# Layers 2 and 3 of a four-layer graph kernel: TensorE bound to the text's order, with timed chains of small steps between the main products

## The chip, the cores and the metric

The kernel runs on one core of a Trainium2 chip. Its time is the device time of one execution in microseconds (us). The kernel before took 2191.8 us in the median of four runs (2189.2 to 2206.82).

## The reference

Four graph layers follow each other on `x` of shape (8, 2048, 64) with one dense 0/1 matrix `adj` of 2048 x 2048. Each layer normalizes its input, applies relu, and adds its result to the input. The change touches layers 2 and 3:

```python
def _L2_gnn_ref(causal_vars, adj_matrix, intervention_value, W1, b1, W2, b2, idx):
    v = causal_vars.at[:, idx].set(intervention_value)
    for _ in range(3):
        effects = jnp.einsum('nm,bmd->bnd', adj_matrix, v)
        h = jnp.concatenate([v, effects], axis=-1)
        h = jax.nn.relu(jnp.einsum('bnk,dk->bnd', h, W1) + b1)
        v = jnp.einsum('bnk,dk->bnd', h, W2) + b2
    return v

def _L3_gnn_ref(x, A, embedding, weight, bias):   # K = 3
    w = jnp.einsum('nd,dkio->nkio', embedding, weight)
    b = jnp.einsum('nd,do->no', embedding, bias)
    As = [eye, A, 2.0 * (A @ A) - eye]
    x_g = jnp.einsum('knm,bmc->bnkc', jnp.stack(As), x)
    return jnp.einsum('bnki,nkio->bno', x_g, w) + b

# layers 2 and 3
h = jnp.maximum(_layernorm(x, axis=-1), 0.0)
x = x + layer(h, adj, ...)
```

## The kernel before

The eight batches are worked in four passes `p` (NP = 4) of two batches, whose 64 features each fill the 128 partitions. The 2048 nodes are the free dimension, cut into four chunks `c` of 512 (`NCW`, `cols(c)`) or sixteen tiles of 128 (NT). The transposed adjacency matrix stays in SBUF as sixteen tiles `aT[m]`.

Everything here happens in `layers23`, from line 1410. A product with the matrix is `spread` (L1482): for one chunk, sixteen tiles times two parts, since the left operand is split into a rounded part `hi` and the rest `lo`, both in a one-pass float type. So one chunk of a product is 32 matmuls of 128x512 into one PSUM tile `acc`.

A pass has three stages.

- Layer 2, three steps over four chunks. A chunk begins with `acc = W1v` (or `Wvc`) times `v` (L1515), then `spread`, then a relu on ScalarE (ACT) that writes the chunk of `v` in place (L1517). In steps 0 and 1 `moved` (L1454) makes the next left operand: four small matmuls into `py` (L1459), a bias on VectorE (DVE, `yb`, L1466), `hi` on ACT (L1467) and `lo` on GpSimd (POOL, L1468). In step 2 the chunk is finished instead: a product with W2 into `pv`, the sum with x, the store of x3 with the bias of layer 3, the normalization (`norm`), and a transpose (`turned`, L1471).
- The first product of layer 3, into `y1`, with a transpose of each chunk.
- The second product of layer 3 into `y2`. After each chunk, its four tiles go through the `u` stage: a transpose `px` of x (L1555), then two groups `w` of six matmuls of 64 rows (L1564). The two batches' matmuls of a pair use different halves of the rows of TensorE. DVE multiplies by the embedding (L1572) and adds (L1576, L1582), POOL folds (L1583 to L1585), SP stores.

Within that last stage `enter` (L1491) begins the next pass for a chunk: load x, mean (L719), subtract, square, variance (L724), logarithm, exponential, multiply, and `moved` with W1e. Chunk c - 1 enters while chunk c is in its `u` stage. Chunk 3 enters after the last `u`. The first pass enters all four chunks before its first step in the text.

`check` (L1433) also tests the matrix: it loads a 128x512 piece `raw` (256 KB) and lets DVE see whether it holds anything but 0 and 1. Two pieces stand at the start of each chunk of layer 2 until all 64 are done.

The text doesn't set the order in which the engines work. A planner puts each engine's instructions in an order by its own estimates of time, and takes later work when earlier work isn't ready by these estimates. Within an engine the order then is fixed, and every engine works its list in turn. `tc.keep_in_program_order` binds an instruction to the place it has in the text; before the change that is done in the `u` stage only, for five of the six matmuls of each group. Buffers rotate within a tag: `x`, `ca` and `fold` have two, `pr` three, `hi` and `lo` six each. A tile that needs a buffer waits until the tile before it in that buffer has been read. DMAs of this part are issued by SP, in order.

Of the kernel before, what the change touches and what calls it, by code (L numbers as in the profile page):

```python
# [16 lines left out]
P = 128  # L17
# [14 lines left out]
def cols(c, w=CW):  # L32
    return slice(c * w, (c + 1) * w)
# [588 lines left out]
class Kit:  # L622


    def __init__(self, tc, t, pool):
        nc = self.nc = tc.nc
        self.tc, self.t = tc, t
        self.ident = pool.tile([P, P], FP, name="ident_f")
# [57 lines left out]
    def layer2_weights(self, pool, ps):  # L686
# [22 lines left out]
        nc.vector.tensor_copy(self.cb, pw)  # L709

    def use_ln_exp(self):
        self.tc.keep_in_program_order(self.nc.scalar.preload_act_table_set(LN_EXP))

    def norm_steps(self, dst, src, mean, var, xc, q):

        nc, mm = self.nc, self.nc.tensor.matmul
        n = dst.shape[-1] // CW
        for c in range(n):
            mm(mean[:, cols(c)], self.avg, src[:, cols(c)], start=True, stop=True)  # L719
        nc.vector.tensor_sub(xc, src, mean)  # L720
        nc.scalar.activation(q, xc, AF.Square)  # L721
        yield
        for c in range(n):
            mm(var[:, cols(c)], self.avg, q[:, cols(c)], start=True, stop=True)  # L724
        nc.scalar.activation(q, var, AF.Ln, bias=self.eps)
        nc.scalar.activation(q, q, AF.Exp, scale=-0.5)
        nc.vector.scalar_tensor_tensor(dst, xc, 0.0, q, op0=OP.max, op1=OP.mult)
        yield
# [679 lines left out]


def layers23(kit, aT, x2_dram, x3_dram, out):  # L1410

    tc, nc, t = kit.tc, kit.nc, kit.t
    mm = nc.tensor.matmul
    ident, ones = kit.ident, kit.ones
    ctx = ExitStack()
    W1v, W1e, W2, Wvc, Wec, cb = kit.W1v, kit.W1e, kit.W2, kit.Wvc, kit.Wec, kit.cb
    b1, b2c, ivc, b1c = kit.b1, kit.b2c, kit.ivc, kit.b1c
    K3, D3 = 3, 16

    fin = ctx.enter_context(tc.tile_pool(name="f_in", bufs=2, reuse_waits="tile"))  # L1420
    w2 = ctx.enter_context(tc.tile_pool(name="w2f", bufs=1, reuse_waits="tile"))
    sb = ctx.enter_context(tc.tile_pool(name="f_sb", bufs=2, reuse_waits="tile"))
    ps = ctx.enter_context(tc.tile_pool(name="f_ps", bufs=2, space=PSUM, reuse_waits="tile"))

    def norm(dst, src):

        mean = ps.tile([P, CW], FP, tag="tp", name="mean")
        var = ps.tile([P, CW], FP, tag="tp", name="var")
        xc = fin.tile([P, CW], FP, tag="ca", name="xc")
        q = fin.tile([P, CW], FP, tag="q", name="q", bufs=1)  # L1430
        kit.norm(dst, src, mean, var, xc, q)

    def check(n):  # L1433

        for _ in range(n):
            if not todo:
                return
            m, h = todo.pop(0)
            a = sb.tile([P, CW], FP, tag="fold", name="raw")
            nc.sync.dma_start(out=a, in_=t["adjT"][m * P : (m + 1) * P, cols(h)])  # L1440
            k = 7 + NCW * m + h
            nc.vector.scalar_tensor_tensor(  # L1442
                a, a, 0.5, a, op0=OP.is_gt, op1=OP.not_equal, accum_out=kit.bad[:, k : k + 1]
            )

    todo = [(m, h) for m in range(NT) for h in range(NCW)]

    def parts():
        return (
            sb.tile([P, 4, P], FR, tag="hi", name="hi", bufs=6),  # L1450
            sb.tile([P, 4, P], FR, tag="lo", name="lo", bufs=6),
        )

    def moved(v, c, W, bias):  # L1454

        py = ps.tile([P, 4, P], FP, tag="tp", name="py")
        for k in range(4):
            m = 4 * c + k
            mm(py[:, k, :], v[:, m * P : (m + 1) * P], W, start=True, stop=True)  # L1459
        hi, lo = parts()  # L1460
        if bias is None:
            nc.scalar.copy(hi, py)
            nc.vector.tensor_tensor(lo, py, hi.bitcast(FP), op=OP.subtract)  # L1463
        else:
            yb = fin.tile([P, 4, P], FP, tag="ca", name="yb")
            nc.vector.tensor_tensor(yb, py, bias[:, None, :].to_broadcast([P, 4, P]), op=OP.add)  # L1466
            nc.scalar.copy(hi, yb)  # L1467
            nc.gpsimd.tensor_tensor(lo, yb, hi.bitcast(FP), op=OP.subtract)  # L1468
        return hi, lo

    def turned(v, c):  # L1471

        tp = ps.tile([P, 4, P], FP, tag="tp", name="tp")
        for k in range(4):
            m = 4 * c + k
            nc.tensor.transpose(tp[:, k, :], v[:, m * P : (m + 1) * P], ident)
        hi, lo = parts()
        nc.scalar.copy(hi, tp)  # L1478
        nc.vector.tensor_tensor(lo, tp, hi.bitcast(FP), op=OP.subtract)  # L1479
        return hi, lo  # L1480

    def spread(acc, y, c, start):  # L1482

        for m in range(NT):
            for part in y[m // 4]:
                mm(acc, part[:, m % 4, :], aT[m][:, cols(c)], start=start, stop=m == NT - 1 and part is y[m // 4][1])  # L1486
                start = False

    v = fin.tile([P, N], FP, name="v", bufs=1)

    def enter(p, c):  # L1491

        xp = fin.tile([P, CW], FP, tag="x", name="xp")
        nc.sync.dma_start(out=xp, in_=x2_dram[p, :, cols(c)])
        norm(v[:, cols(c)], xp)
        if c == 0:
            nc.vector.tensor_copy(v[:, 0:1], ivc)
        return moved(v, c, W1e, None)

    y = [enter(0, c) for c in range(NCW)]  # L1500
    W3 = w2.tile([P, K3, D3 * F], FP, name="W3f")
# [5 lines left out]
    nc.vector.tensor_sub(W3[:, 0, :], W3[:, 0, :], W3[:, 2, :])  # L1507
    nc.vector.tensor_scalar(W3[:, 2, :], W3[:, 2, :], 2.0, None, op0=OP.mult)
    for p in range(NP):
        for step in range(3):  # L1510
            yn = []
            for c in range(NCW):
                acc = ps.tile([P, CW], FP, tag="acc", name="acc")
                check(2)
                mm(acc, Wvc if step else W1v, v[:, cols(c)], start=True, stop=False)  # L1515
                spread(acc, y, c, False)
                nc.scalar.activation(v[:, cols(c)], acc, AF.Relu, bias=b1c if step else b1)  # L1517
                if step < 2:
                    yn.append(moved(v, c, Wec, cb))
                    continue  # L1520
                pv = ps.tile([P, CW], FP, tag="tp", name="pv")
                mm(pv, W2, v[:, cols(c)], start=True, stop=True)
                xp = fin.tile([P, CW], FP, tag="x", name="xq")
                nc.sync.dma_start(out=xp, in_=x2_dram[p, :, cols(c)])
                nc.vector.scalar_tensor_tensor(xp, pv, b2c, xp, op0=OP.add, op1=OP.add)
                bq = sb.tile([P, CW], FP, tag="pr", name="bq", bufs=3)
                nc.sync.dma_start(out=bq, in_=kit.bias_dram[:, cols(c)])
                nc.gpsimd.tensor_add(bq, bq, xp)
                nc.sync.dma_start(out=x3_dram[p, :, cols(c)], in_=bq)
                norm(v[:, cols(c)], xp)  # L1530
                yn.append(turned(v, c))
            y = yn


        y1 = sb.tile([P, N], FP, tag="y1", name="y1", bufs=1)
        yn, after = [], []
        for c in range(NCW):
            acc = ps.tile([P, CW], FP, tag="acc", name="acc")
            spread(acc, y, c, True)
            nc.scalar.copy(y1[:, cols(c)], acc)  # L1540
            yn.append(turned(y1, c))
        for c in range(NCW):
            acc = ps.tile([P, CW], FP, tag="acc", name="acc")
            spread(acc, yn, c, True)
            y2 = fin.tile([P, CW], FP, tag="ca", name="y2")
            nc.scalar.copy(y2, acc)
            xp = fin.tile([P, CW], FP, tag="x", name="xr")
            nc.sync.dma_start(out=xp, in_=x3_dram[p, :, cols(c)])
            if c > 0 and p + 1 < NP:
                after.append(enter(p + 1, c - 1))  # L1550
            for k in range(4):
                i = 4 * c + k
                ns, ks = slice(i * P, (i + 1) * P), slice(k * P, (k + 1) * P)
                px = ps.tile([P, P], FP, tag="tp", name="px")
                nc.tensor.transpose(px, xp[:, ks], ident)  # L1555
                xs = sb.tile([P, 2, F], FP, tag="xs", name="xs", bufs=1)
                nc.scalar.copy(xs.rearrange("p h f -> p (h f)"), px)
                pr = []
                for w in range(2):
                    u = [ps.tile([P, 8, F], FP, tag=f"u{h}", name=f"u{h}") for h in range(2)]  # L1560
                    for kk, src in enumerate((v[:, ns], y1[:, ns], y2[:, ks])):
                        for h in range(2):

                            one = mm(  # L1564
                                u[h].rearrange("p d o -> p (d o)"), src[half(h), :], W3[half(h), kk, cols(w)],
                                start=kk == 0, stop=kk == 2,
                            )
                            if kk or h:
                                tc.keep_in_program_order(one)
                    for h in range(2):  # L1570
# [6 lines left out]
                        else:  # L1577
                            pr.append(a)
                fold = sb.tile([P, 2, 4, F], FP, tag="fold", name="fold")
                ot = sb.tile([P, 2, F], FP, tag="ot", name="ot", bufs=1)  # L1580
# [7 lines left out]
                )  # L1588
        y = after + [enter(p + 1, NCW - 1)] if p + 1 < NP else None
    ctx.close()  # L1590
# [101 lines left out]
```

## Time and profile before

| | |
|---|---|
| median of four runs | 2191.8 us |
| the profiled execution | 2197.11 us, span 2195.3 us |
| mean granted TensorE clock | 0.981 |
| layers 2 and 3 | from about 993 us to the end |
| last `u` stage's end | about 2184 us |
| raw checks (DVE) | 24 in pass 0, 24 in pass 1, 16 in pass 2, none in pass 3 |

The starts of the first W1v product of the four passes are at 1006.5, 1312.4, 1610.8 and 1907.5 us.

How to read the lines that follow: a row of a group of instructions gives line, engine, operation, output and inputs, shapes and count, then busy time and mean ns of one, then the idle time before. A row of waits gives the waiting instruction, the one it waited for, the total in us, the number of times, and the longest. A row of a stretch gives its borders, its length, the busy time and number of instructions of TensorE (PE), its weight load, DVE, ACT and POOL, then the granted clock, the share of the DMA engines and GB/s. A row of the timeline gives start, length, engine, line, operation, names and shapes, and in brackets the idle time before with what ended it.

### The profile page before, as it was taken

The page shows a single profiled execution, that of the slowest core. Times are in us where ns is not written, and L with a number is a line of the kernel's source. Part 1 is how long each engine was busy: PE and PEld are TensorE (multiplying, and loading weights), DVE is VectorE, ACT ScalarE, POOL GpSimd, SP SyncE. Part 2 cuts the span into 40 slices and gives each one's busy share as a digit, 9 for nine tenths or more (in the row PEclk, how much of TensorE's full clock was granted, in tenths as well). Part 3 has the DMA queues.
Part 4 walks back from the last instruction along what each step waited for, and adds up shares of the span by engine and source line. Part 5 has one row for each costly group of instructions (what it writes and reads, how often), then busy time and mean ns, then how long its engine had stood idle before and what let it go on. Part 6 is the DMA issues. An engine that isn't in the chain of part 4 may idle for free.

```text
span 2195.3 us, 23784 instructions
## 1 busy us (share of the span) xinstructions
PE 2097.5 (96%) x9164; PEld 1158.3 (53%) x9164; DVE 1219.5 (56%) x1890; ACT 451.7 (21%) x852; POOL 297.5 (14%) x416
## 2 busy tenths in 40 slices
PE   7999898888999999998999999999999999999997
PEld 4777655423222222225766547774557664576653
DVE  6675588868888887874223564116551235501265
ACT  4322244464111111002121111120111201112100
POOL 0211154301000000000110121101111011111022
PEclk9999899989999999999999999999999999999999
DMA  4665361154111111104210014000030100101000
GB/s 122 195 202 154 118 212 45 52 164 154 44 34 39 58 34 39 49 20 135 65 43 8 22 37 122 24 20 21 24 100 6 44 10 21 42 1 34 11 19 12
DMA packets 86154, 140.26 MB, mean 64 GB/s; under 512 B 33040, under 2 KB 33296, under 8 KB 83792
## 3 DMA queue, kind: packets, MB, share of 16 engines
q1 hardware_dynamic: 67984, 88.05, 13.5%
q0 software_dynamic: 18048, 50.60, 7.6%
q8 instruction: 74, 1.21, 0.2%
q14 instruction: 48, 0.39, 0.1%
HBM read 107.89 MB, written 30.74 MB: 63 GB/s over the span
## 4 chain that ended last, share of the span: by engine, by line
PE 63%; issue 16%; DVE 6%; DMA 6%; POOL 4%; ACT 2%; POOLq 0%; DVEq 0%; SPq 0%; ACTq 0%
PE acc L1486 19%; PE o L1355 11%; PE u L1564 7%; PE dn L1361 6%; DMA raw<-in_adjT 3%; PE acc L913 2%; PE var L724 2%; PE pgs L1141 2%; PE py L1459 2%; PE mean L719 2%; PE acc L1515 1%; POOL fold L1583 1%; DVE ex L1139 1%; POOL mix L1140 1%; PE ph L1302 1%
## 5 line engine op out<-in xcount | busy, mean ns | idle before, releaser
L1486 PE MATMUL acc<-aT,hi 128*128 128x512 f32 x960 | 402.1, 419 | 0.0
L1486 PE MATMUL acc<-aT,lo 128*128 128x512 f32 x960 | 388.7, 405 | 0.0
L1355 PE MATMUL o<-pt,hS 128*64 128x512 f32 x1024 | 269.9, 608 | 5.8 <-DVE pt L1370 5.8
L1370 DVE SCALAR_TENSOR_TENSOR pt<-R,wd,aT 128x1024 f32<-128x1024 f32 x192 | 239.1, 1280 | 41.4 <-PE dn L1361 22.9
L1564 PE MATMUL u<-W3f,y 64*128 64x512 f32 x1024 | 258.3, 592 | 0.0
L1572 DVE TENSOR_TENSOR pr<-u,embf 128x512 f32<-128x512 f32 x256 | 171.5, 688 | 123.0 <-PE u L1564 110.9
L1486 PEld LDWEIGHTS acc<-aT,hi 128*128 128x128 f32 x960 | 181.0, 189 | 62.1 <-issue 23.5
L1486 PEld LDWEIGHTS acc<-aT,lo 128*128 128x128 f32 x960 | 180.9, 188 | 51.2 <-issue 13.6
L1355 PEld LDWEIGHTS o<-pt,hS 128*64 128x64 f32 x1024 | 70.8, 137 | 188.5 <-issue 174.8
L1564 PEld LDWEIGHTS u<-W3f,y 64*128 64x128 f32 x1024 | 104.4, 187 | 124.6 <-issue 124.6
L1564 PE MATMUL u<-W3f,v 64*128 64x512 f32 x512 | 146.5, 617 | 0.0
L1361 PE MATMUL dn<-pt,vd 128*32 128x512 f32 x1024 | 142.4, 599 | 0.0
L913 PE MATMUL acc<-at,Y 128*128 128x512 f32 x512 | 134.9, 408 | 2.3 <-DVE ev L922 2.3
L1486 PE MATMUL acc<-aTl,lo 128*128 128x512 f32 x320 | 129.7, 406 | 6.2 <-DVE lo L1463 4.5
L1486 PE MATMUL acc<-aTl,hi 128*128 128x512 f32 x320 | 128.4, 402 | 3.4 <-ACT hi L1467 3.4
L1583 POOL TENSOR_TENSOR fold<-fold 128x256 f32<-128x256 f32 x64 | 47.3, 739 | 556.2 <-DVE fold L1582 556.2
L1466 DVE TENSOR_TENSOR yb<-py,cb_f 128x512 f32<-128x512 f32 x32 | 22.1, 690 | 160.7 <-PE py L1459 160.6
L913 PEld LDWEIGHTS acc<-at,Y 128*128 128x128 f32 x512 | 94.0, 192 | 25.1 <-issue 4.2
L721 ACT ACTIVATE q<-xc 128x512 f32<-128x512 f32 (+1 forms) x56 | 38.7, 691 | 266.7 <-DVE xc L720 253.9
L1576 DVE TENSOR_TENSOR pr<-pr 128x512 f32<-128x512 f32 x128 | 88.1, 689 | 2.2
L1479 DVE TENSOR_TENSOR lo<-tp,hi 128x512 fp32r<-128x512 f32 x32 | 22.1, 692 | 117.5 <-ACT hi L1478 117.5
L1442 DVE SCALAR_TENSOR_TENSOR raw<-raw 128x512 f32<-128x512 f32 x64 | 49.1, 772 | 68.9 <-DMA raw<-in_adjT 68.6
(278 smaller groups left out, 2718.7 us busy)
## 6 DMA issues: line engine op xcount, KB each, us to landing
at<-in_adjT POOLq DMA_DIRECT2D x32, 512.0 KB, 4.6
raw<-in_adjT SPq DMA_DIRECT2D x64, 256.0 KB, 3.2
aT<-in_adjT POOLq DMA_DIRECT2D x12, 1024.0 KB, 7.1
R<-r_dram SPq DMA_DIRECT2D x14, 512.0 KB, 3.6
hi_dram<-hi SPq DMA_DIRECT2D x16, 264.0 KB, 2.7
lo_dram<-lo SPq DMA_DIRECT2D x16, 264.0 KB, 3.5
hhi<-hi_dram POOLq DMA_DIRECT2D x16, 264.0 KB, 3.0
hlo<-lo_dram POOLq DMA_DIRECT2D x16, 264.0 KB, 3.1
```

What stands on the lines that cost most here:

```text
L719: mm(mean[:, cols(c)], self.avg, src[:, cols(c)], start=True, stop=True)
L724: mm(var[:, cols(c)], self.avg, q[:, cols(c)], start=True, stop=True)
L913: mm(acc[p], Y[h][:, m, p, :], at[:, k, :], start=m + h == 0, stop=m == NT - 1 and h == 1)
L1355: mm(o[half(b2), cols(k)], hS[:, m, half(b2)], pts[b2][:, cols(k)], start=m == 0, stop=m == NT - 1)
L1361: mm(dn[q : q + 32, :], vd[:, m, b2 : b2 + 1].to_broadcast([P, 32]), pts[b2][:, cols(k)], start=m == 0, stop=m == NT - 1, tile_position=(0 ...
L1370: nc.vector.scalar_tensor_tensor(pt, R[b2], wd[:, m, b2 : b2 + 1], aT[m][:, s].bitcast(FP), op0=OP.max, op1=OP.mult)
L1442: nc.vector.scalar_tensor_tensor(a, a, 0.5, a, op0=OP.is_gt, op1=OP.not_equal, accum_out=kit.bad[:, k : k + 1])
L1486: mm(acc, part[:, m % 4, :], aT[m][:, cols(c)], start=start, stop=m == NT - 1 and part is y[m // 4][1])
L1564: one = mm(u[h].rearrange("p d o -> p (d o)"), src[half(h), :], W3[half(h), kk, cols(w)], start=kk == 0, stop=kk == 2,)
L1572: nc.vector.tensor_tensor(a, u[h], emb[:, i, 8 * w : 8 * w + 8, None].to_broadcast([P, 8, F]), op=OP.mult)
L1576: nc.vector.tensor_add(pr[h], pr[h], a)
L1583: nc.gpsimd.tensor_add(fold[:, :, 0:2, :], fold[:, :, 0:2, :], fold[:, :, 2:4, :])
```

## The change

Every matmul and transpose of layers 2 and 3 goes through `kit.mm` or `kit.turn`, which bind it to the text's order. To make that order, the text is now written by a small clock, `Weave`: the work between main products (entering, carrying, leaving, turning) is written as generators, `chains`, that yield the time after which their next step may stand. `spread` and the `u` stage tell the clock how long they take (0.47 us for two matmuls, 0.93 for the W product, 0.27 and 2.8 in the `u` stage), and steps that are due are put into the text there. `until` puts steps in at once until an operand exists.

Besides this:

- `moved` makes `lo` on DVE in all cases, no longer on POOL where there is a bias.
- `hi` and `lo` of chunks 2 and 3 take buffers of `fold` and `pr` (`LENT`) for the operands made in step 0 and step 2.
- The raw pieces use the two buffers of `x` instead of `fold`, and stand in steps 0 and 1 alone, so 16 in each pass.
- Mean and variance use PSUM of `u0`, `u1` (at the start and in step 2) or of `acc` (in the `u` stage). The tile `q` is gone; the normalization writes into its own output.
- The first pass enters all four chunks before the first product; chunks 2 and 3 are loaded into y1's space.
- In the last chunk's `u` stage the next pass's chunk 3 enters too, in parts of `y1` that are no longer read; after the stage ACT copies it into `v`.
- The first product of layer 3 takes its first two chunks together, tiles 0 to 7, 8 to 11, 12 to 15 of each in turn.
- x for `leave` and for the `u` stage is loaded ahead of the chunk's product.

```diff
+    def mm(self, *args, **kw):
+        one = self.nc.tensor.matmul(*args, **kw)
+        if self.strict:
+            self.tc.keep_in_program_order(one)
...
+class Weave:
+    def __init__(self):
+        self.now, self.chains = 0.0, []
+    def start(self, chain):
+        self.chains.append([self.now + next(chain), chain])
+    def step(self, c):
+        d = next(c[1], None)
+        if d is None:
+            self.chains.remove(c)
+        else:
+            c[0] = self.now + d
+    def passed(self, us):
+        self.now += us
+        for c in list(self.chains):
+            if c[0] <= self.now:
+                self.step(c)
+    def until(self, there):
+        while not there():
+            c = min(self.chains, key=lambda c: c[0])
+            self.now = max(self.now, c[0])
+            self.step(c)
...
-            a = sb.tile([P, CW], FP, tag="fold", name="raw")
+            a = fin.tile([P, CW], FP, tag="x", name="raw")
...
+    LENT = (None, None, ("fold", 2), ("pr", 3))
...
-            nc.gpsimd.tensor_tensor(lo, yb, hi.bitcast(FP), op=OP.subtract)
...
+        nc.scalar.copy(hi, py)
+        nc.vector.tensor_tensor(lo, py, hi.bitcast(FP), op=OP.subtract)
...
+    def normed(dst, src, tags, xc=None):
+        mean = ps.tile([P, CW], FP, tag=tags[0], name="mean")
+        mm(mean, kit.avg, src, start=True, stop=True)
+        xc = fin.tile([P, CW], FP, tag="ca", name="xc") if xc is None else xc
+        nc.vector.tensor_sub(xc, src, mean)
+        nc.scalar.activation(dst, xc, AF.Square)
+        yield 3.5
+        var = ps.tile([P, CW], FP, tag=tags[1], name="var")
+        mm(var, kit.avg, dst, start=True, stop=True)
+        nc.scalar.activation(dst, var, AF.Ln, bias=kit.eps)
+        nc.scalar.activation(dst, dst, AF.Exp, scale=-0.5)
+        nc.vector.scalar_tensor_tensor(dst, xc, 0.0, dst, op0=OP.max, op1=OP.mult)
+        yield 3.5
+    def spread(acc, y, c, start, ms):
+        for m in ms:
+            weave.until(lambda: y[m // 4] is not None)
+            for h, part in enumerate(y[m // 4]):
+                mm(acc, part[:, m % 4, :], aT[m][:, cols(c)], start=start, stop=m == NT - 1 and h == 1)
                 start = False
+            weave.passed(0.47)
...
+    def enter(c, y, xp, delay, tags, at=None):
+        yield delay
+        src, k = (v, c) if at is None else (at, 1)
+        yield from normed(src[:, cols(k)], xp, tags, at if at is None else at[:, cols(2)])
         if c == 0:
             nc.vector.tensor_copy(v[:, 0:1], ivc)
+        y[c] = moved(src, k, W1e, None)
+    def carry(c, step, yn):
+        yield 1.4
+        yn[c] = moved(v, c, Wec, cb, None if step else LENT[c])
+    def leave(p, c, xp, yn):
+        yield 1.4
+        pv = ps.tile([P, CW], FP, tag="tp", name="pv")
+        mm(pv, W2, v[:, cols(c)], start=True, stop=True)
...
+        yield 1.8
+        yield from normed(v[:, cols(c)], xp, ("u0", "u1"))
+        yn[c] = turned(v, c, LENT[c])
+    def again(y1, c, yn):
+        yield 1.4
+        yn[c] = turned(y1, c)
+    kit.strict = True
+    y = [None] * NCW
+    room = sb.tile([P, N], FP, tag="y1", name="room", bufs=1)
+    for c in range(NCW):
+        xp = chunk_of(x2_dram[0], c) if c < 2 else load(room[:, cols(c)], x2_dram[0], c)
+        weave.start(enter(c, y, xp, 2.0 * c, ("u0", "u1")))
+    weave.until(lambda: not weave.chains)
...
                 acc = ps.tile([P, CW], FP, tag="acc", name="acc")
-                check(2)
+                if step < 2:
+                    check(2)
+                else:
+                    xp = chunk_of(x2_dram[p], c)
                 mm(acc, Wvc if step else W1v, v[:, cols(c)], start=True, stop=False)
-                spread(acc, y, c, False)
+                weave.passed(0.93)
+                spread(acc, y, c, False, every)
                 nc.scalar.activation(v[:, cols(c)], acc, AF.Relu, bias=b1c if step else b1)
...
+                weave.start(carry(c, step, yn) if step < 2 else leave(p, c, xp, yn))
...
+        two = [ps.tile([P, CW], FP, tag="acc", name="acc") for c in range(2)]
+        for ms in (range(0, 8), range(8, 12), range(12, NT)):
+            for c in range(2):
+                spread(two[c], y, c, 0 in ms, ms)
+                if NT - 1 in ms:
+                    nc.scalar.copy(y1[:, cols(c)], two[c])
+                    weave.start(again(y1, c, yn))
...
             if c > 0 and p + 1 < NP:
-                after.append(enter(p + 1, c - 1))
+                weave.start(enter(c - 1, after, xp, 0.0, ("acc", "acc")))
+                if c == LAST:
+                    xp = load(y1[:, cols(0)], x2_dram[p + 1], c)
+                    weave.start(enter(c, after, xp, 2.0, ("acc", "acc"), y1))
...
+                    weave.passed(2.8)
...
-        y = after + [enter(p + 1, NCW - 1)] if p + 1 < NP else None
+        if p + 1 < NP:
+            weave.until(lambda: None not in after)
+            nc.scalar.copy(v[:, cols(LAST)], y1[:, cols(1)])
+        y = after
```

## The prediction

> **What bounds the kernel now.** I read the page from the top, then asked the trace only for the stage that the diff touches. The first row of the page says which engine matters; the digits of slices 19 to 40, which are layers 2 and 3, stand at 9 almost throughout.
>
> ```profile
> PE 2097.5 (96%) x9164; PEld 1158.3 (53%) x9164; DVE 1219.5 (56%) x1890; ACT 451.7 (21%) x852; POOL 297.5 (14%) x416
> ...
> L1486 PE MATMUL acc<-aT,hi 128*128 128x512 f32 x960 | 402.1, 419 | 0.0
> L1564 PE MATMUL u<-W3f,y 64*128 64x512 f32 x1024 | 258.3, 592 | 0.0
> ```
>
> The engine is TensorE, and a gain here can only be time in which it stands, runs at a lower clock, or does its work in a worse order. "Busy" hides the last two, so next I took starts from the timeline: 32 product matmuls start 0.2333 us apart (7.47 us per chunk), a 128x512 fp32 matmul takes 0.94 us, the eight records of `py` 0.91 us. Then I asked what TensorE waited for between 1017 and 2186 us:
>
> ```profile
> PE var L724 <- ACT q L721: 4.9, 12, 0.5
> PE acc L1486 <- DVE lo L1463: 4.5, 3, 2.4
> PE acc L1486 <- ACT hi L1467: 3.4, 2, 1.9
> PE acc L1486 <- POOL lo L1468: 1.7, 2, 0.8
> ```
>
> These lines and three smaller ones (3.1 us) make 17.6 us in all, the most that plain waits can return behind the start. The rest must come from clock and order, which stretches of equal work show:
>
> ```profile
> 1063.37:1070.20 6.83, 6.07 (x15) 4.32 (x16) 2.59 (x7) 0.69 (x1) 0.71 (x1) 0.50 0.38 131
> 1363.75:1367.16 3.41, 3.41 (x8) 2.74 (x9) 1.19 (x4) 0.00 (x0) 0.00 (x0) 0.50 0.27 79
> ...
> 1623.16:1626.57 3.41, 3.02 (x7) 2.44 (x8) 1.04 (x3) 0.00 (x0) 0.00 (x0) 0.50 0.62 153
> ...
> 2099.43:2129.37 29.94, 29.94 (x134) 15.46 (x133) 18.63 (x32) 1.55 (x5) 6.56 (x12) 1.00 0.08 18
> ...
> 1247.12:1282.07 34.95, 34.31 (x146) 17.21 (x145) 20.69 (x35) 4.08 (x9) 6.54 (x12) 1.00 0.09 23
> ```
>
> The number after the engines is the granted clock: three stretches at 0.50 follow waits. The last two rows are the same work (one chunk's second product and four tiles of `u`) without and with one `enter` of the next pass woven in: 5.0 us apart.
>
> **The change part by part, against the profiled execution (2197.1 us, 5.3 above the median).**
>
> *Order in the `u` stage.* The `enter` itself needs, from starts in place (1249.07, 1251.53, 1254.82 us), 0.95 us for the mean, 1.06 for the variance, 1.00 for `py`: 3.0 us. The other 2.1 us are 0.38 + 0.25 to 0.44 us of waiting, and pairs pulled apart: normally the two 64-row matmuls of a pair start 6 ns apart, but between 1221.06 and 1224.69 us the planner mixed `v` and `y` products of two groups and the halves follow each other. Bound to the text, the three steps stand between whole groups, 5.6 us apart (the chain asks for 3.5, and the next point after that is a full tile later), while mean to variance needs 2.5 us and variance to `py` 3.5 here. Nine such chunks (three in each of three passes): 9 x 2.1 = 19 us. Between px and `u` a normal switch costs 0.26 us, so I leave 0.3 for each `enter`: 16 us gained.
>
> *The last chunk entered in y1.* Today chunk 3 enters after the last `u`, since `v` is still read; TensorE then waits 0.48 + 1.51 us (1315, 1322), 0.48 + 2.39 us plus 3.02 us of work at half clock (1614 to 1626), and 0.48 us (1911): 6.9 us with 1.5 for the clock. All of it goes; its 3.0 us of matmuls stay, earlier. One `ACT` copy (0.58 us by the y row) is added, needed only three chunks later (28 us), so it costs nothing; without that cover it would cost 0.6 us each. Less three switches: 6 us gained.
>
> *Step 0 to step 1.* At 1060.5 and 1360.5 us TensorE waits 1.94 + 0.84 and 1.49 + 0.85 us, then works 6.07 and 3.41 us at half clock (3.0 and 1.7 lost): 9.8 us. The timeline says why:
>
> ```profile
> 1360.39 0.69 DVE L1442 SCALAR_TENSOR_TENSOR raw<-raw 128x512 f32<-128x512 f32 x1 [1.21 <-DMA raw<-in_adjT]
> ...
> 1361.00 0.69 DVE L1466 TENSOR_TENSOR yb<-py,cb_f 128x512 f32<-128x512 f32 x1
> ```
>
> `py` was done at 1355.05; `yb` stands behind raw checks that wait for their DMAs (3.2 us each) and comes 6 us late. The change puts 16 checks in each pass instead of 24, 24, 16, 0. At the present rate, one in 2.0 us, 16 end within 32 us, before the boundary 37 us into the pass. Moving `lo` from POOL (1.29 us) to DVE (0.69) shortens the same chain by 0.6 and loads DVE, which is idle there (0.69 us busy in a chunk of 9.44 without checks). I take the whole 10 us; were checks still running at the boundary, none of it.
>
> The Trainium skill speaks against that price ("TensorE: Matmul & The Clock Gate", "The HAM clock gate"): the clock falls after at least one idle window of about 3.4 us, so waits of 2.3 us would cost themselves only, and by that the sum would be 23 instead of 28. The rows above show 0.50 after 2.34 and 2.39 us of waiting, so the term stays.
>
> *Lent buffers.* The new `hi` and `lo` of chunks 2 and 3 no longer wait for the old ones. No wait on such a release stands among TensorE's waits: 0.
>
> *The start.* All four chunks now enter before the first product. Step 1 begins at 1053.15 today; 36.4 us of step 0 (four times 0.94 + 7.47, three `py`) put the equivalent start at 1016.8. The variance of chunk 0 can't come before 998.54 (ACT is on layer 1's tail). From there four enters are 11 us at full clock, and about 4 more while the clock is at 0.50: the last `py` ends between 1011 and 1015, if the two x loads into y1's space are there. Unknown: that space may come free only when layer 1 ends. Bounds -2 and +6 us; I take +3, in the middle, since xp loads land in 2.9 us and can hide behind chunks 0 and 1.
>
> *New waits.* A bound TensorE can't fill a late operand. Slots against present distances: relu to `py` 1.64 us given, 1.17 needed; pv to mean 2.8 against 2.0; mean to variance 4.4 against 2.5; variance to transpose 4.4 against 3.3. Only the last transpose before y1's last quarter is tight: about 1.4 us stand between it and the first use, hi and lo need 1.5 and 2.15: 0.5 us x 4 = 2 us lost. Worse, the checks now share `x`, whose buffers come free within the last chunk's `u` stage, and the planner sends loads as soon as a buffer is free. DVE needs 18.6 us already for four tiles that take TensorE 22.5, plus two enters (4.2 us); each check adds 0.77 us and a wait (68.6 us over 51 today, 1.35 each). None that slips in costs 0; six in each of three passes are 12.7 us less about 4 us of slack, 27 us in all. I take 5, near the low end, because the checks come behind `u` in the text.
>
> Sum: 16 + 6 + 10 + 3 - 2 - 5 = **28 us**. 2197.1 - 28 = 2169 for an execution like the profiled one; on the median, 2191.8 - 28 = **2164 us**.
>
> **Rivals.**
> *Nothing new in the way* (0.15): no check slips in, the start gives its +6: 16 + 6 + 10 + 6 - 2 = 36, and 2 to 4 more if the enters cost no switch: 2152 us. For it: POOL and ACT are nearly idle. Against it: 51 DVE waits for raw loads today.
> *Order gives nothing* (0.25): if the 1.4 us per `enter` beyond its waits are the price of full-row matmuls between half-row ones and not of broken pairs, only 0.7 x 9 = 6 us of the first term remain. Then 6 + 6 + 10 + 3 - 7 = 18, or 8 if the checks keep the boundary stall: about 2179 us. That is the case in which the binding doesn't do what it says. For it: the rows at 1218 to 1225 don't separate the two.
> *Slower* (0.15): the raw checks pace DVE under a bound TensorE. Place: the last `u` stage of three passes (27 us) and the step 0 to 1 boundary of all four (6 us each, the lateness at 1361), every one followed by a half-clock stretch (1.7 us x 7 = 12): 63 lost against 37 gained, 2191.8 + 26 = 2218 us. It decides once the checks cost over 37 us. For it: SP issues in order, and a raw load waiting for its buffer holds the `out` stores behind it. Against it: fewer checks per pass.
> Forecast: 0.45.
>
> **How the numbers follow.** Two kernels less than 1% (22 us) apart can hardly be told apart here: 2170 and 2214 are the bounds. The forecast spreads over 2154 to 2176 by its unknown terms. Faster by over 1%: all of the first rival and 0.33 of the forecast, 0.48. Within: 0.12 of the forecast, 0.24 of the second, 0.05 of the last, 0.41. Slower: 0.11. The range of 2147 to 2207 leaves out about one in ten on either side.
>
> **What the profile after would show.** Chunks with an enter at 32.9 to 33.5 us instead of 35; no TensorE wait for `q` in the `u` stage; no stretch at 0.50 after 1015 us; DVE waiting for raw loads without TensorE behind it. Wrong would be: TensorE's waits for `pr` or `fold` in the last chunk, a late `yb`, or the first product after 1017 us.

## The result, and the profile after

The changed kernel takes 2201.2 us in the median of 52 runs, the kernel before 2195.3 in 78: ratio 1.0022, 95% interval 1.0015 to 1.003. It is a little slower, where 2164 us was forecast. The top of the page of the changed kernel:

```profile
span 2199.2 us, 23688 instructions
...
PE 2082.4 (95%) x9164; PEld 1168.3 (53%) x9164; DVE 1229.6 (56%) x1922; ACT 451.6 (21%) x855; POOL 260.5 (12%) x384
```

The same 9164 matmuls take 15 us less busy time than before (2097.5) in a span 3.9 us longer. So the work did get denser, and TensorE waits more. Who it waits for between 1017 and 2186 us, in the view of waits (total, times, longest):

```profile
PE py L713 <- DVE lo L1503: 18.3, 3, 6.1
PE u L713 <- DVE pr L1660: 4.7, 7, 1.1
PE px L719 <- ACT xs L1646: 1.5, 3, 0.5
PE py L713 <- DVE v L1529: 1.4, 2, 1.2
PE acc L713 <- DVE lo L1514: 1.1, 4, 0.3
PE acc L713 <- ACT hi L1513: 1.0, 4, 0.2
```

The waits for `hi` and `lo` at the step ends are gone (the last two rows are the four tight places in y1). A new one stands on top, three times, once in each pass that has a successor. The stretches show where: the third chunk's period with an enter, the last chunk of pass 0, and two half-clock stretches (columns as before: busy time of PE, PEld, DVE, ACT, POOL, then granted clock, DMA share, GB/s).

```profile
1246.10:1278.80 32.70, 32.70 (x146) 16.96 (x145) 20.33 (x35) 4.08 (x9) 6.55 (x12) 1.00 0.09 25
1278.80:1321.40 42.60, 34.25 (x126) 14.37 (x124) 24.73 (x53) 6.04 (x12) 4.80 (x7) 0.92 0.24 72
1306.60:1313.40 6.80, 5.71 (x18) 3.43 (x20) 4.49 (x10) 0.75 (x2) 2.02 (x3) 0.50 0.17 51
...
1897.10:1907.30 10.20, 6.13 (x18) 3.65 (x20) 7.32 (x16) 0.75 (x2) 2.01 (x3) 0.50 0.22 66
```

A chunk with an enter takes 32.7 us instead of 35.0, a little less than the 32.9 to 33.5 forecast. The last chunk takes 42.6, from the first transpose of its `u` stage to the next pass's first product. DVE executes 53 instructions there, and its own waits in that stretch point to the checks:

```profile
DVE raw L1480 <- DMA raw<-in_adjT: 16.3, 7, 3.1
DVE xc L1522 <- PE mean L713: 5.0, 1, 5.0
```

Eleven of the next pass's checks stand in DVE's list inside the last `u` stage. DVE spends 16.3 us there waiting for their loads, with the work that TensorE needs behind them. The timeline shows the first load going out as soon as `xc` has read an `x` buffer, and then the worst place:

```profile
1279.94 0.69 DVE L1522 TENSOR_TENSOR xc<-xp,mean 128x512 f32<-128x512 f32 x1 [5.01 <-PE mean L713]
...
1280.66 16.20 SPq L1478 DMA_DIRECT2D raw<-in_adjT  x5
...
1299.53 0.69 DVE L1480 SCALAR_TENSOR_TENSOR raw<-raw 128x512 f32<-128x512 f32 x1 [1.83 <-DMA raw<-in_adjT]
1299.60 0.57 ACT L1502 CAST hi<-py 128x512 fp32r<-128x512 f32 x1
...
1303.28 0.69 DVE L1480 SCALAR_TENSOR_TENSOR raw<-raw 128x512 f32<-128x512 f32 x1 [2.44 <-DMA raw<-in_adjT]
...
1306.95 0.69 DVE L1503 TENSOR_TENSOR lo<-py,hi 128x512 fp32r<-128x512 f32 x1
...
1307.69 2.08 PE L713 MATMUL py<-W1e_f,y 128*128 128x128 f32 x8 [6.10 <-DVE lo L1503]
```

`lo` of chunk 2 frees the PSUM buffer that `py` of chunk 3 needs. Its `hi` was ready at 1300.2, it runs at 1306.95, and TensorE, bound to put `py` next, stands 6.1 us and then works at half clock.

Why the checks come so early now is argued, not shown. Before, with the pieces in `fold`, none stands in a last `u` stage; with order alone (below), still in `fold`, it is 1, 1 and 0. So the `x` buffers, free early in that stage, are the likely reason; the changed kernel with its pieces back in `fold` was not run.

### The profile page after: what moved, and what is told of

Same layout as the page of the kernel before. It is cut to its first block, busy times and chain, and to the rows that moved or that the text cites. A ratio compares the mean times of both kernels' runs of the same rounds, so it can differ in the third digit from the quotient of the medians.

```text
span 2199.2 us, 23688 instructions
## 1 busy us (share of the span) xinstructions
PE 2082.4 (95%) x9164; PEld 1168.3 (53%) x9164; DVE 1229.6 (56%) x1922; ACT 451.6 (21%) x855; POOL 260.5 (12%) x384
## 4 chain that ended last, share of the span: by engine, by line
PE 54%; issue 28%; DVE 6%; DMA 5%; POOL 3%; ACT 1%; POOLq 0%; SPq 0%; DVEq 0%; ACTq 0%
PE acc L713 28%; PE u L713 10%; PE acc L925 2%; DMA raw<-in_adjT 2%; PE pgs L1153 2%; PE py L713 2%; PE mean L713 1%; PE var L713 1%; DVE ex L1151 1%; POOL mix L1152 1%; PE pf L1204 1%; DMA at<-in_adjT 1%; PE tp L719 1%; PE pv L713 1%; DVE raw L1480 1%
## 5 line engine op out<-in xcount | busy, mean ns | idle before, releaser
L713 PE MATMUL acc<-aT,hi 128*128 128x512 f32 x960 | 419.5, 437 | 0.0
L713 PE MATMUL acc<-aT,lo 128*128 128x512 f32 x960 | 380.0, 396 | 0.0
L1382 DVE SCALAR_TENSOR_TENSOR pt<-R,wd,aT 128x1024 f32<-128x1024 f32 x192 | 239.1, 1280 | 40.9 <-PE dn L1373 25.1
L713 PE MATMUL u<-W3f,y 64*128 64x512 f32 x1024 | 249.8, 596 | 0.0
L713 PEld LDWEIGHTS acc<-aT,hi 128*128 128x128 f32 x960 | 180.6, 188 | 65.6 <-issue 29.2
L1480 DVE SCALAR_TENSOR_TENSOR raw<-raw 128x512 f32<-128x512 f32 x64 | 44.2, 691 | 75.7 <-DMA raw<-in_adjT 75.2
L1382 DVE SCALAR_TENSOR_TENSOR pt<-R,wd,aTl 128x1024 f32<-128x1024 f32 x64 | 80.1, 1282 | 7.6 <-PE dn L1373 4.0
L1646 ACT COPY xs<-px 128x128 f32<-128x128 f32 x64 | 17.1, 267 | 321.8 <-POOL ot L1674 259.0
```

The lines of the kernel that those rows point to most:

```text
L713: one = self.nc.tensor.matmul(*args, **kw)
L1382: nc.vector.scalar_tensor_tensor(pt, R[b2], wd[:, m, b2 : b2 + 1], aT[m][:, s].bitcast(FP), op0=OP.max, op1=OP.mult)
L1480: nc.vector.scalar_tensor_tensor(a, a, 0.5, a, op0=OP.is_gt, op1=OP.not_equal, accum_out=kit.bad[:, k : k + 1])
```

## The experiments

The first mean of layer 2 starts anywhere between 990.7 and 999.1 us in the profiled executions of these kernels, so next to times I compare stages of the profiles. Ratios are to runs of the kernel before taken beside each experiment (medians 2192.9 to 2193.6 us); most have four runs and intervals of 0.2 to 0.4% to either side, so medians a few us apart are not told apart. "Start" is from the first mean of layer 2 to the first product of step 1 in pass 0 (before: 60.1 us, changed: 64.9). "Last chunk" is from the first transpose of the fourth chunk's tiles to the next pass's first product (changed: 42.6, 42.2, 42.4 us in passes 0 to 2). A pass is from first product to first product.

**The checks bound to the text's order on DVE** (label checks_bound):

```diff
-            nc.vector.scalar_tensor_tensor(
+            one = nc.vector.scalar_tensor_tensor(
                 a, a, 0.5, a, op0=OP.is_gt, op1=OP.not_equal, accum_out=kit.bad[:, k : k + 1]
             )
+            tc.keep_in_program_order(one)
```

> The changed kernel with one thing added: the 64 raw checks on VectorE are bound to the text's order too, so none can stand ahead of the u stage's work; their loads stay free to come early. Theory A (checks taken early hold VectorE, and through it TensorE, in the last u stage of passes 0 to 2; two early raw loads hold SP's list before the room loads at the start): the last chunk falls from 42 us to 35 to 36 us, no TensorE wait for lo of about 6 us, the first product moves from 1024.5 to about 1018 us, ratio to the kernel before 0.987 to 0.992. Theory B (the last chunk is slow since two enters share it: acc, tp and VectorE's time; the room loads wait for layer 1's space): last chunk stays above 40 us, first product at 1024, ratio 1.000 to 1.003.

2162.1 us, ratio 0.9848 (0.9808 to 0.9888). The last chunk takes 29.2 us in all three passes, 13.2 less on average, so both enters fit into it. Its stretch (1281.4 to 1310.5) has no half clock and 21 DVE instructions fewer:

```profile
1281.40:1310.50 29.10, 28.87 (x125) 12.12 (x123) 18.79 (x32) 6.16 (x12) 4.90 (x9) 1.00 0.08 23
```

I had expected 35 to 36 us, having counted the chunk's product into this stretch, which stands before it; the ratio too is better than expected. Theory B is out for the last chunk. The start stays at 64.6 us, so that part of theory A is not confirmed by this run: the room loads (of x for chunks 2 and 3, into y1's space) are issued 7.2 us after the first mean instead of 10.9, two raw loads still stand ahead of them, and TensorE still waits 5.1 us for them (9.3 in the changed kernel).

**Their loads bound on SP as well** (label checks_and_loads_bound):

```diff
-            nc.sync.dma_start(out=a, in_=t["adjT"][m * P : (m + 1) * P, cols(h)])
+            tc.keep_in_program_order(nc.sync.dma_start(out=a, in_=t["adjT"][m * P : (m + 1) * P, cols(h)]))
```

> The changed kernel with checks and their loads bound to the text's order on VectorE and on SP. Theory A: as with the checks alone, the first product perhaps 1 us earlier, and a loss of at most 3 us in a pass where the first checks of a pass now wait for late loads; ratio 0.986 to 0.993. Theory B: ratio 1.000 to 1.003.

2153.1 us, ratio 0.9811 (0.9771 to 0.985), better than expected and the lowest median of all, though others lie within its interval. Start 62.1 us, passes 1 and 2 283.5 us, and between 1025 and 2145 us TensorE waits for hardly anything:

```profile
PE acc L713 <- DVE lo L1515: 1.1, 4, 0.3
PE acc L713 <- ACT hi L1514: 1.0, 4, 0.2
PE py L713 <- DVE lo L1504: 0.7, 3, 0.2
```

**The loads alone bound** (label loads_bound): the edit on SP just shown, without the one on DVE.

> The changed kernel with the raw loads alone bound on SP; the checks are free on VectorE. A load then can't be issued before the last tile's store, so no check can come early: the last chunk's u stage is as short as with both bound (29 to 30 us from its first transpose to the next pass's first product), ratio 0.981 to 0.987. If the checks find another early place, 33 us or more.

2155.6 us, 0.9819 (0.9779 to 0.9859); last chunk 29.2 us. Either binding removes the early checks, and with them the loss.

**No checks at all**, in the changed kernel and in the one before (labels after_without_checks and before_without_checks): `todo = []`.

> The changed kernel without the test of the matrix: no raw load, no check (the flags of these pieces stay zero); all else is computed. Theory A: the floor of the changed order: last chunk 35 to 36 us, first product 1016 to 1018, no half-clock stretch between 1015 us and the end of the last pass, ratio 0.984 to 0.990. Theory B: ratio not under 0.996, last chunk above 40 us.

2161.1 us, 0.9844 (0.9797 to 0.9892). Last chunk 29.2 us, passes 1 and 2 283.6: the checks themselves cost nothing where their place is right. The start is 64.9 us, as long as with checks. There the loads of x for step 2 take the free `x` buffers early, and stand ahead of the room loads in the place of the raw loads. My 1016 to 1018 for the first product was missed (1021.3), as were the 35 to 36 us of the last chunk, and a half-clock stretch at 1018.6 was left.

> The kernel before without the test of the matrix. If its stalls at 1060, 1322, 1360 and 1620 us come from checks that wait for loads, they go: 16 to 20 us, ratio 0.991 to 0.993. If they come from the planner's order of TensorE itself, under 5 us go, ratio 0.998 or more. Against the changed kernel without checks it shows what order and weaving alone are worth: by my prediction's terms about 16 to 20 us.

2180.4 us, 0.9933 (0.9915 to 0.9952). Steps 0 and 1 of passes 1 and 2 fall to 39.0 and 37.8 us, from 40.8 and 42.1, 43.1 and 37.8: the stalls of the kernel before are gone, for 13 us in the medians and 17 from the first mean to the last `u`, where I had expected 16 to 20. Without checks the changed kernel is 19 us faster than the one before (2161.1 against 2180.4).

**The checks bound in the kernel before** (label before_checks_bound): both bindings, nothing else.

> The kernel before with its 64 checks and their loads bound to the text's order on VectorE and SP, nothing else. Theory A (the checks' place in VectorE's list made the stalls at 1060, 1322, 1360 and 1620 us, not the checks themselves): these stalls go as they did without checks, ratio 0.991 to 0.995, no half-clock stretch between 1020 and 2160 us. Rival (the checks must cost that somewhere): 0.998 or more.

2179.7 us, 0.9933 (0.991 to 0.9955), the same stage lengths as without checks. So the place of the checks cost the kernel before 0.7%, and two lines undo it without any weaving. Against this kernel, order and weaving with bound checks gain a further 27 us (2153.1 against 2179.7).

**Order alone** (label order_alone): in the kernel before, every matmul and transpose of layers 2 and 3 bound, the text as it was.

```diff
-    mm = nc.tensor.matmul
+    mm = kit.mm
+    kit.strict = True
...
-            nc.tensor.transpose(tp[:, k, :], v[:, m * P : (m + 1) * P], ident)
+            kit.turn(tp[:, k, :], v[:, m * P : (m + 1) * P])
```

> The kernel before with all TensorE instructions of layers 2 and 3 bound to the text's order, and the text left as it was: no chains. By the distances in the trace of before each small step then waits for its operand in place: about 1.2 us after each of 32 chunks, about 9 us in each of 16 chunks of step 2, 6 us in each of 16 enters, and half-clock work behind each: 300 to 450 us slower, ratio 1.13 to 1.2. If order alone were the gain, the ratio would be under 1.

2441.4 us, 1.1127 (1.1071 to 1.1183); the gap was expected at 300 to 450 us and is 248. The stage from step 2 to the first `u` tile takes 123 to 126 us a pass instead of 87, and these four kinds of wait make 143 us of the loss:

```profile
PE var L713 <- ACT q L733: 56.2, 32, 3.8
PE tp L719 <- DVE v L739: 34.7, 16, 2.2
PE py L713 <- ACT v L1530: 26.1, 32, 1.1
PE py L713 <- DVE v L739: 26.1, 12, 2.3
```

All waits of TensorE in layers 2 and 3 sum to about 190 us; the mean clock of the execution falls from 0.981 to 0.940. In this kernel the binding is worth having only with the chains that fill these places.

**Layer 3's weight prepared later** (label start_w3_late), on top of both bindings. In the run with checks and loads bound, DVE waited for this weight's load ahead of chunk 3's enter.

```diff
-    nc.vector.tensor_sub(W3[:, 0, :], W3[:, 0, :], W3[:, 2, :])
-    nc.vector.tensor_scalar(W3[:, 2, :], W3[:, 2, :], 2.0, None, op0=OP.mult)
+    def weights3():
+        tc.keep_in_program_order(nc.vector.tensor_sub(W3[:, 0, :], W3[:, 0, :], W3[:, 2, :]))
+        tc.keep_in_program_order(nc.vector.tensor_scalar(W3[:, 2, :], W3[:, 2, :], 2.0, None, op0=OP.mult))
...
+            if p == 0 and step == 1:
+                weights3()
```

> Checks and loads bound, and besides the two VectorE instructions that prepare layer 3's weight are bound behind step 0 of the first pass. In the run with checks and loads bound the first of them stood ahead of chunk 3's enter and waited for its load: TensorE's py of chunk 3 waited 3.8 us. Theory A (VectorE's list holds work that waits for late loads ahead of what TensorE needs): the first product comes 3 to 4.5 us earlier against the first mean, 20.5 to 22 us after it instead of 25.1; 2149 to 2150 us where checks and loads bound alone take 2153. Rival (the half clock and ACT's queue set the start): under 1 us.

The first product comes 21.2 us after the first mean instead of 25.1, the start falls to 57.2 us. The time is 2154.2 us, 0.981 (0.9786 to 0.9833), no better than without the edit, where I had expected 2149 to 2150: the profiled execution reached layer 2 about 4.5 us later. The cause is shown by the stage; the gain in time is not.

**The first product after chunk 0 alone** (label start_overlapped), with the late weight: `weave.until(lambda: y[0] is not None)`.

> As before, and the first product of pass 0 may stand after chunk 0 has entered; chunks 1 to 3 enter between its matmuls. My prediction's price of the start took the four enters in a row as equal to the planner's overlap. If the row itself costs, step 1 begins 3 to 7 us earlier against the first mean than with all four in a row; if TensorE would only wait inside the first product instead, within 1.5 us of it, or later.

Start 61.5 us, 4.3 longer than with four enters in a row; 2156.4 us, 0.9822 (0.9799 to 0.9844). TensorE waits inside the first product for `lo` (2.2 us) and `hi` (1.4) and falls to half clock at 1023 us. Letting the first product begin early doesn't shorten the start.

**Chunk 3 enters after the last u** (label last_chunk_after), on both bindings:

```diff
-                if c == LAST:
-                    xp = load(y1[:, cols(0)], x2_dram[p + 1], c)
-                    weave.start(enter(c, after, xp, 2.0, ("acc", "acc"), y1))
...
-            weave.until(lambda: None not in after)
-            nc.scalar.copy(v[:, cols(LAST)], y1[:, cols(1)])
+            xp = chunk_of(x2_dram[p + 1], LAST)
+            weave.start(enter(LAST, after, xp, 0.0, ("u0", "u1")))
```

> Checks and loads bound, but chunk 3 of the next pass enters after the last u, woven into step 0's first chunk, not in y1's space. My prediction gave the early entering 2 us a pass, 6 in all. Expected: the three passes 1 to 3 us longer each, 2156 to 2162 us. Rival (the 12 tiles of the first product hide a chain of 9 us wherever it stands): within 0.5 us a pass.

2160.3 us, 0.9836 (0.9812 to 0.986). Of the 6.2 us that its profile is longer than that of the run with checks and loads bound, most lies outside the passes: from step 1 of pass 0 to the last `u` it is 1087.5 us against 1086.0. Passes 1 and 2 take 284.1 us instead of 283.5. So y1's space is worth about 0.5 us a pass, as the rival said.

**No lent buffers** (label no_lending), on both bindings: all four entries of `LENT` are `None`.

> Checks and loads bound, without the lent buffers: hi and lo of all chunks in their own six. My prediction gave the lending nothing. Expected: stage lengths within 0.3 us, time within 0.1%. Rival (in TensorE's fixed order a late buffer is a stall): 0.5 to 2 us in each of steps 0 and 2, 4 to 16 us in all.

Behind the start the stages agree within 0.2 us (passes 1 and 2 283.4), and the start is 63.0 us against 62.1; 2156.5 us, 0.9838 (0.9804 to 0.9872). Nothing shows a gain by lending.

**`lo` on POOL again** (label lo_on_pool), with bindings and late weight: the engine of `lo` is `nc.gpsimd` where there is a bias.

> Checks, loads and weight preparation bound as in the run with the late weight; lo of the carried chunks is made on GpSimd again (1.29 us instead of 0.69). My prediction took 0.6 us off the chain at each step's end with it. Expected: stages within 0.3 us and time within 0.1%, since the chain has about 2.6 us to spare; rival: 0.6 us at each of 8 step ends and checks held by GpSimd, 5 us or more.

2154.8 us, 0.9821 (0.9782 to 0.9861); all stages within 0.1 us. The move to DVE gives nothing and costs nothing.

## Why the prediction was wrong

The mechanism was described and its price was wrong. Under new waits I wrote that checks could slip into the last `u` stage, bounded that at 0 to 27 us, and took 5, "because the checks come behind `u` in the text". That is the step that failed: the text's order says nothing about an engine that isn't bound to it. Eleven checks of each pass slip in, not six, and the last chunk is 13.2 us longer three times, 40 us in all. Above the bound of 27 lie the count and the half-clock stretches, which I had priced only in the last rival; by the term's own formula eleven checks would have made (11 x 2.12 - 4) x 3 = 58 us, so it was the count that failed and not the price of a check. With the checks bound and nothing else changed, the time is 2162 us, against a forecast of 2164. That nearness is partly luck: the start came out 7 to 8 us worse than its term, and 12 us of gain stood in no term.

Term by term, from stages of the profiles; "undisturbed" is the run with checks and loads bound.

| term | forecast us | measured us |
|---|---|---|
| order in the `u` stage | +16 | +18.3, the move of chunk 3 included: from a pass's first `px` to step 1 of the next 167.5 us before with checks bound, 160.4 undisturbed, three times, less 0.9 each for the steps |
| last chunk in y1's space | +6 | +5.8, all of it check stalls in step 0 of passes 1 and 2; the space itself 1.5, within the row above |
| step 0 to step 1 | +10 | +10.2: step 1 of passes 0 and 1 from 43.7 and 42.1 to the 37.8 it has without checks |
| start | +3 (bounds -2, +6) | -4.8; -2.0 undisturbed; +2.9 with the late weight |
| y1's tight places | -2 | -2.1 |
| checks in the last `u` stage | -5 (bounds -27, 0) | -39.7 |
| lent buffers, `lo` on DVE | 0 | 0 |
| not seen: steps and y1 | 0 | +12.3: 0.23 us in each of 28 chunks of steps 0 and 1, 1.5 in the rest of each pass |

The measured column adds up to nothing, and so do the stages: from the first mean of layer 2 to the end of the last `u` it is 1190.7 us before and 1190.4 after. The 3.9 us between the two spans lie outside, 2.5 before the first mean and 1.7 behind the last `u`. So the profiles show why the gain is missing; why the medians are 5.9 us apart they don't show.

**Order in the u stage.** Right in cause, though waits and pulled-apart pairs were not told apart; all of the 2.3 us per chunk went and the 0.3 I held back for switches isn't there: a chunk with an enter now takes 2.7 us more than one without (32.63 against 29.93). The first of each pass's three was not 35.0 but 36.9 us before. The rival that order gives nothing is out.

**Last chunk.** The stalls of before at 1322 and 1620 us stood under this term. They were the checks' again; in the kernel before, `lo` stands behind two of them:

```profile
1322.24 0.69 DVE L1442 SCALAR_TENSOR_TENSOR raw<-raw 128x512 f32<-128x512 f32 x1 [2.99 <-DMA raw<-in_adjT]
...
1322.86 0.69 DVE L1442 SCALAR_TENSOR_TENSOR raw<-raw 128x512 f32<-128x512 f32 x1
...
1323.48 0.69 DVE L1463 TENSOR_TENSOR lo<-py,hi 128x512 fp32r<-128x512 f32 x1
```

Without checks, and with them bound, pass 1's step 0 falls from 40.8 to 39.0 us and pass 2's from 43.1 to 39.0, with chunk 3 still entering after the last `u`. I had read the waiting instruction (`lo`) and not what stood ahead of it in DVE's list, though I did just that for step 0 to 1.

**Start.** Outside its bounds, and I had named a reason: y1's space. In the undisturbed run the room loads wait 10.9 us for the last operations of layer 1 on DVE and are issued 6.3 us after the first mean; in the changed kernel it is 10.9 us after it, since four raw loads stand ahead of them on SP:

```profile
999.97 6.46 SPq L1478 DMA_DIRECT2D raw<-in_adjT  x4
1006.48 0.95 SPq L1542 DMA_DIRECT2D room<-xd  x2
```

In the undisturbed run they stand first:

```profile
1000.87 0.80 SPq L1543 DMA_DIRECT2D room<-xd  x2
```

That the raw loads are not all of it was shown by the run without checks, where other early loads do the same. The late weight removes 4.9 us of what is left; the rest of the start was not split. The first product after 1017 us (1024.5) was one of my signs of being wrong, and so were TensorE's waits for `pr` in the last chunk.

**Slower.** This rival had the place and about two thirds of the price: 40 us in the last `u` stages with the half clock, where it put 27 and three stretches of 1.7, and nothing at the boundaries of step 0, where it put 24 and four stretches. Its 37 us of gain, the point at which it decides, doesn't follow from the forecast's terms, which make 33 without the checks (16 + 6 + 10 + 3 - 2). The stages gained 39.7 us and lost 39.7, so it ended in a tie: the start lost 8 us against my sum and the steps gained 12. That the median of 2201 lies within the range up to 2207 is luck, the balance of errors that oppose each other.

**Clock.** The waits of 6.1 us are followed by 6.8, 6.8 and 10.2 us at 0.50. In every run the half-clock stretches are 3.4, 6.8, 10.2 or 13.7 us long, but for the one behind the last `u`, which the end of the program cuts. The Trainium skill ("TensorE: Matmul & The Clock Gate", "The HAM clock gate") gives a free-running window of 3.41 us, which agrees with these lengths; its idle of one whole window before the fall does not agree with the 2.3 us waits of the kernel before, and the measured fall decides.

## What to carry to other kernels

Binding one engine to the text's order moved the question to the lists of the others. Work that depends on nothing but a load is what this planner takes early, and while the load is not there, everything behind it on that engine waits. So here that work had to be bound too, or it sat where the bound engine couldn't step around it. When a stall names an instruction, look at what stands just ahead of it in the same engine's list before giving it a cause of its own.

## What the runs showed of the hardware

In steps 0 and 1 a group of small fp32 matmuls directly behind an fp32 product cost more than the same group after two one-pass matmuls. In the kernel before, the planner put `py` right behind the W product. From the start of the W product to the second product matmul behind `py` it took 2.24 us there (1984.33 to 1986.57); with two more product matmuls between, 2.46 us (1916.52 to 1918.98), of which they are 0.47 by their usual distance. That is about 0.25 us less for the same work. A whole chunk of step 1:

```profile
1984.33:1993.77 9.44, 9.44 (x43) 7.21 (x42) 0.69 (x1) 1.31 (x2) 1.29 (x1) 1.00 0.00 0
```

is one of the kernel before, and of the run with checks and loads bound:

```profile
1916.50:1925.70 9.20, 9.20 (x43) 7.29 (x42) 2.61 (x6) 1.31 (x2) 0.00 (x0) 1.00 0.19 57
```

Both have the same 43 records at full clock and differ by 0.24 us. Why the pair cost more was not tried.
